# One expert product moved within the step of a fused attention and expert-mixture kernel

## Chip, cores and metric

The kernel runs on one NeuronCore of a Trainium2 chip. The metric is the device time of one execution in microseconds (us), as a median over runs; a separate profiled execution gives the trace. The engines are TensorE (PE: matrix products, with its weight loads shown as PEld), VectorE (DVE), ScalarE (ACT), GpSimd (POOL) and SyncE (SP, which here issues the DMAs). Each has its own queue and works it in order; engines meet through semaphores.

## What is computed

The input x is 2 images of 128 channels x 256 x 256 pixels in float32. One layer has two halves. The first is a dilated halo attention with four heads of 32 channels: in each window of 8 x 8 pixels the queries see a 12 x 12 surrounding, and a fixed mask leaves only the keys of the same parity. The second is a mixture of eight linear experts, of which the router takes two for each pixel.

```python
# attention half, on the channel-normalised x
qkv = einsum('bchw,oc->bohw', ln_c(x), W_qkv)
attn = softmax(q * SCALE @ k.T + rel_pos_emb(q) + FIXED_MASK)   # per window and head
x = x + einsum('bchw,oc->bohw', attn @ v, W_out)
# expert half, on every pixel as a token t of 128 channels
probs = softmax(ln_t(t) @ router_w + router_b)
top_p, top_i = top_k(probs, 2); top_p = top_p / sum(top_p)
t = t + sum_k top_p[k] * (ln_t(t) @ expert_w[top_i[k]] + expert_b[top_i[k]])
```

The kernel computes all eight experts for every pixel and multiplies each expert's input by its gate, which is zero for the six experts not taken; the eight products are summed in PSUM.

## The kernel before

An image is cut into strips of eight pixel rows, 64 strips for both images. The parity mask splits a strip into four planes (even or odd rows, even or odd columns) of 512 pixels, and attention is done plane by plane: 256 planes. The main loop (L779) has one step n for each plane and seven more to finish the experts. Within the loop the order of every engine's instructions is the order in which the Python code issues them (`manual_schedule`, L778); nothing is reordered afterwards.

A step interleaves four different pieces of work at different stages of a pipeline:
- `scores` (L436) and `attend` (L477) of plane n: the keys product (line 448, which adds position terms and mask) and the scores (line 465) into the PSUM tile `att`, an exponential on ACT (`pT`, line 473), sums (line 486) and weighted values (line 496), and on DVE a division that gives `o` (line 516).
- `project` (L357) of plane n+1, called `ahead` in the loop: first half of the values (`pvv`, line 369), position terms (`pu`, line 384), keys (`pk`, line 396), queries (`pq`, line 418), and later the second half of the values. The inputs come from the normalised strip `xn` and from window columns `xcol`, which POOL copies.
- `out_project` (L520) of plane n: the output product `po` (line 524), then on DVE the sum with the strip (line 529).
- `norms`, `route` and `spread` for a group of 512 pixels of the strip before: sums of squares by PE (line 554), a transpose `plg` and small operations on DVE, ACT's exponential (line 592), the choice of two experts by rank, and a write of the gates to DRAM (`gd`).

The experts belong to the class `Experts` (L644). `fetch` (L652) lets SP read a gate row back, broadcast over 128 partitions (256 KB), into a buffer `gb`; a one-column write on DVE or ACT ahead of it makes the DMA wait for the buffer. `times` (L673) multiplies the centred pixels `xs` with the gate and gives `xe`, for experts 0 to 4 and 6 on DVE and for 5 and 7 on POOL. `product` (L683) is the matmul of expert e into the PSUM tile `acc`, with 512 columns; in float32 it is two weight loads and two matmuls in the trace. `end` (L690) adds `acc` to the strip on DVE. `acc` has one buffer; `xe` has eight.

One group of 512 pixels spreads its eight products over two steps. In step n, after the second half of the values, come products 0, 1 and 2 (L848 to L851), then `po` (L862), then product 3 (L863). In step n+1, after keys, scores, first values, `pu`, `pk` and `pq`, come products 4, 6, 7 and 5 (L817). The variable `ex` is the group whose products run; it is replaced by the next group at L841, after the four products and `end`.

At the head of each step from the seventh on, L793 pads PE's instructions with idle ones, so that the step begins at a fixed place within a block of 256 instructions (`BLOCK` 256, `FIRST_LIMIT` 95, L47): the first 95 instructions of a step fall into one block and the next block begins after them. Small PSUM products share three buffers (`ps_mm`, L88).

Of the kernel before, what the change touches and what calls it, by code (L numbers as in the profile page):

```python
# [51 lines left out]
def kernel(  # L52
# [383 lines left out]
    def scores(n, state):  # L436


        qs, kk, au = state["qs"], state["kk"], state["au"]
        turn = place(n // 4, 0) // 2  # L440
        att = ps_att.tile([P, 4, 512], F32, tag="att", name=f"att{n}")
        sc = att[:, :, 0:HQ]
        for w in range(2):
            for half in range(2):
                rows = slice(half * SLOT, (half + 1) * SLOT)
                for h in range(HEADS):
                    hp = slice(h * DH, (h + 1) * DH)
                    nc.tensor.matmul(
                        sc[rows, h].rearrange("p (t w z) -> p t w z", w=2, z=16)[:, :, w],
                        lhsT=keys[hp, turn, w],  # L450
                        rhs=au[hp, half * NP + w : (half + 1) * NP : 2].rearrange(
                            "p t a s -> p t (a s)"
                        ),
                        start=(w == 0),
                        stop=False,
                    )
        for t in range(HP):
            if t == HP // 2:
                yield
            for half in range(2):  # L460
                rows = slice(half * SLOT, (half + 1) * SLOT)
                m0 = 2 * (half * HP + t)
                for h in range(HEADS):
                    hp = slice(h * DH, (h + 1) * DH)
                    nc.tensor.matmul(  # L465
                        sc[rows, h, 32 * t : 32 * t + 32],
                        lhsT=kk[hp, half * HP + t, :],
                        rhs=qs[hp, m0 : m0 + 2].rearrange("p m a s -> p (m a s)"),
                        start=False,
                        stop=(t == HP - 1),  # L470
                    )
        pT = work.tile([P, HEADS, HQ], F32, tag="pT", name=f"pT{n}", bufs=1)
        nc.scalar.activation(pT, att[:, :, 0:HQ], AF.Exp)  # L473
        state.update(att=att, pT=pT)
        yield

    def attend(n, state):  # L477


        att, pT, vv = state["att"], state["pT"], state["vv"]  # L480
        av = att[:, :, HQ:512]
        for half in range(2):
            rows = slice(half * SLOT, (half + 1) * SLOT)
            for h in range(HEADS):
                hp = slice(h * DH, (h + 1) * DH)
                nc.tensor.matmul(
                    av[hp, 2 + half], lhsT=ones[rows, :], rhs=pT[rows, h], start=True, stop=True
                )
        for t in range(HP):
            if t == HP // 2:  # L490
                yield
            for half in range(2):
                rows = slice(half * SLOT, (half + 1) * SLOT)
                for h in range(HEADS):
                    hp = slice(h * DH, (h + 1) * DH)
                    nc.tensor.matmul(  # L496
                        av[hp, half, 32 * t : 32 * t + 32],
                        lhsT=vv[rows, t, hp],
                        rhs=pT[rows, h, 32 * t : 32 * t + 32],
                        start=True,  # L500
                        stop=True,
                    )


        sT = work.tile([P, 2, HQ], F32, tag="sT", name=f"sT{n}", bufs=1)
        nc.vector.transpose(sT, av[:, 2:4])
        rc = small.tile([P, NQ // 32], F32, tag="rc", name=f"rc{n}")
        nc.vector.reciprocal(rc, sT.rearrange("p f (b k) -> p (f b) k", k=32)[:, :, 0])
        yield
        rT = work.tile([P, 2, HQ], F32, tag="rT", name=f"rT{n}", bufs=1)  # L510
        nc.vector.transpose(
            rT.rearrange("p f (b k) -> p (f b) k", k=32),
            rc.unsqueeze(2).broadcast_to([P, NQ // 32, 32]),
        )
        o = work.tile([P, 2, HQ], F32, tag="o", name=f"o{n}")
        nc.vector.tensor_tensor(o, av[:, 0:2], rT, ALU.mult)  # L516
        state["o"] = o
        yield

    def out_project(n, state):  # L520

        i, pl = divmod(n, 4)
        po = mm_tile(f"po{n}")
        nc.tensor.matmul(  # L524
            po, lhsT=wo, rhs=state["o"].rearrange("p f z -> p (f z)"), start=True, stop=True
        )
        yield
        xv = xt[i].rearrange("p (a y) (m s x) -> p y x m a s", y=2, x=2, s=4)[:, pl // 2, pl % 2]
        nc.vector.tensor_add(xv, po.rearrange("p (m a s) -> p m a s", a=PR, s=4), xv)
        yield  # L530
# [188 lines left out]
    def store(i, k):  # L719
        b, s = strips[i]  # L720
        r = s * R + 2 * k
        nc.sync.dma_start(out[b, :, r : r + 2, :], xt[i][:, 2 * k : 2 * k + 2, :])
        if k == R // 2 - 1:
            xt.pop(i)
# [48 lines left out]
    gated, ex, nxt = None, NoExperts(), NoExperts()  # L773
# [4 lines left out]
    with tc.manual_schedule(engines={ET.PE, ET.DVE, ET.Activation, ET.Pool, ET.SP}):  # L778
        for n in range(n_planes + 7):  # L779
            i, pl = divmod(n, 4)  # L780
            score, attn, outp, ahead, norm, rout = none, none, none, none, none, none
            if n < n_planes:
                score = scores(n, states[n])
                attn = attend(n, states[n])
                outp = out_project(n, states[n])
            if n + 1 < n_planes:
                states[n + 1] = {}
                ahead = project(n + 1, states[n + 1])

            if 6 <= n < n_planes:
                nc.tensor.addr_align(BLOCK, offset=BLOCK - FIRST_LIMIT)  # L793


            next(score, None)
            new, row = NoExperts(), None
            if gated and gated[0]:
                rout = route(*gated[0], *gated[2])
            next(rout, None)  # L800
            nxt.fetch(5, nc.scalar)
            for _ in rout:
                pass
            next(score, None)
            next(ahead, None)
            nxt.fetch(7, nc.scalar)
            if gated:
                f, c, made = gated
                gd, rb1 = spread(f, c, made[0], f"_{n}")
                row = (*c, rb1) if c else None  # L810
                new = Experts(*f, gd) if f else new
            next(ahead, None)
            if n + 1 < n_planes:
                states[n + 1]["shift"]()
            next(ahead, None)
            next(ahead, None)
            for e in (4, 6, 7, 5):  # L817
                ex.product(e)


            f = (i - 1, pl) if 0 < i <= len(strips) else None
            c = row_at(n)
            if f or c:
                norm = norms(f, c, f"_{n}")
            next(norm, None)
            next(attn, None)
            nxt.means()
            new.fetch_means()
            for e in (0, 1, 2, 3):
                nxt.times(e, dve)  # L830
            new.fetch(0, dve)
            for e in (4, 6):
                nxt.times(e, dve)
            new.fetch(1, dve)
            ex.end()
            new.fetch(2, dve)
            next(attn, None)
            next(attn, None)


            ex = nxt  # L841
            next(norm, None)
            load_x((n + 9) // 4, (n + 9) % 4, paced=True)
            new.fetch(3, dve)
            while to_store:
                store(*to_store.pop())
            next(ahead, None)
            ex.product(0)  # L848
            made = next(norm, None)
            ex.product(1)  # L850
            ex.product(2)  # L851
            new.fetch(4, nc.scalar)
            nxt.behind(6)
            nxt.times(5, pool)
            if row:
                ln1(*row, pool)
            if pl == 3 and i + 2 < len(strips):
                halo(i + 2)
            nxt.times(7, pool)
            if n + 2 < n_planes:  # L860
                columns(n + 2)
            next(outp, None)  # L862
            ex.product(3)  # L863
            next(outp, None)
            new.fetch(6, dve)
            gated, nxt = (f, c, made) if made else None, new
            states.pop(n, None)
# [58 lines left out]
```

The softmax here doesn't subtract the row's maximum and nothing guards it: scores larger than these inputs give would overflow.

## Time and profile before

| What | us |
|---|---|
| Median of 4 runs | 4485.49 |
| Lowest and highest of them | 4482.61, 4487.03 |
| The profiled execution's own time | 4482.61 |
| Its span in the trace | 4480.8 |
| PE busy | 4422.0 |
| DVE busy | 3997.3 |
| ACT busy | 1468.9 |
| POOL busy | 1319.7 |

The span is the time from the first to the last instruction in the trace. "Busy" is the time in which an engine had at least one instruction under way; ends of matmuls are modelled, so PE's figure is not the share of its peak. The granted PE clock was 0.998 on average. The timeline of one step shows the start in us from the span's start, the length of a merged group, engine, line, operation and tiles, and how many instructions were merged (two for each float32 product). One step, from the keys product of one plane to that of the next, goes from 2002.25 to 2019.41 us: 17.16 us. In it DVE is busy for 15.81 us, ACT for 5.87 us and POOL for 5.21 us.

The list of waits gives, for an instruction group, what it waited for, the total time, the number of waits and the longest. Lines with "issue" are times in which an engine waited for nothing that the trace shows. An instruction-queue line (q8) counts the packets with which the program itself is fetched.

### The profile page before, as it was taken

How to read it: one execution, taken by the hardware profiler on the slowest of the kernel's cores; microseconds unless marked ns; L12 is line 12 of the kernel's file. 1: busy time of each engine (PE TensorE's matmuls, PEld its weight loads, DVE VectorE, ACT ScalarE, POOL GpSimd, SP SyncE). 2: the span in 40 equal slices, each digit the busy share in tenths (PEclk: the TensorE clock that was granted, in tenths of full speed). 3: DMA queues.
4: the chain of work that ended last, by engine and by line, in shares of the span. 5: the costliest groups of instructions: out<-in, count | busy, mean ns of one | idle time of the engine just before them, and what ended most of it. 6: DMA issues, size and time to landing. Idle time of an engine off the chain costs nothing. (4 is left out here: it accounts for less than half of the span.)

```text
span 4480.8 us, 224632 instructions
## 1 busy us (share of the span) xinstructions
PE 4422.0 (99%) x96321; PEld 2681.4 (60%) x96321; DVE 3997.3 (89%) x11850; ACT 1468.9 (33%) x4022; POOL 1319.7 (29%) x1815
## 2 busy tenths in 40 slices
PE   7999999999999999999999999999999999999997
PEld 5666666666666666666666666666666666666653
DVE  5899999999999999999989999999999999999887
ACT  3333333333333333333333333333333333333321
POOL 1232323232323232332323232323232323232321
PEclk9999999999999999999999999999999999999999
DMA  2566666666656666666666666666666666666656
GB/s 82 176 191 185 192 184 192 185 192 185 193 184 193 184 192 185 191 188 189 187 188 187 189 188 188 190 185 192 184 193 185 192 183 194 186 192 184 192 164 187
DMA packets 519284, 828.12 MB, mean 185 GB/s; under 512 B 124186, under 2 KB 125850, under 8 KB 518298
## 3 DMA queue, kind: packets, MB, share of 16 engines
q1 hardware_dynamic: 517568, 813.46, 60.1%
q8 instruction: 769, 12.60, 1.1%
q14 instruction: 217, 1.78, 0.2%
q10 hardware_dynamic: 730, 0.29, 0.0%
HBM read 737.95 MB, written 75.56 MB: 182 GB/s over the span
## 5 line engine op out<-in xcount | busy, mean ns | idle before, releaser
L686 PE MATMUL acc<-xe,ew 128*128 128x512 f32 x4096 | 1890.0, 594 | 19.5 <-DVE gb L660 18.2
L686 PEld LDWEIGHTS acc<-xe,ew 128*128 128x128 f32 x4096 | 758.0, 190 | 887.4 <-issue 862.7
L677 DVE TENSOR_TENSOR xe<-xs,gb 128x512 f32<-128x512 f32 x1536 | 950.5, 686 | 11.2 <-PE acc L686 1.4
L681 POOL COPY last<-xe 128x1 f32<-128x1 f32 x256 | 48.3, 189 | 3058.2 <-DVE gb L660 3051.1
L376 ACT COPY vv<-pvv 128x512 f32<-128x512 f32 x512 | 300.2, 586 | 1396.4 <-PE pvv L369 1380.5
L677 POOL TENSOR_TENSOR xe<-xs,gb 128x512 f32<-128x512 f32 x512 | 651.1, 1273 | 5.6 <-PE att L496 2.1
L369 PE MATMUL pvv<-wt,xcol 128*128 128x128 f32 x4096 | 594.0, 288 | 2.5 <-POOL xcol L331 1.5
L369 PEld LDWEIGHTS pvv<-wt,xcol 128*128 128x128 f32 x4096 | 496.2, 191 | 64.7 <-issue 51.8
L272 POOL TENSOR_TENSOR xn<-xt,rb 128x512 f32<-128x512 f32 x249 | 375.2, 1507 | 69.1 <-DMA rb<-gd 60.6
L465 PE MATMUL att<-qs,kcol 32*64 32x32 f32 x32768 | 391.6, 226 | 1.0 <-issue 1.0
L465 PEld LDWEIGHTS att<-qs,kcol 32*64 32x64 f32 x32768 | 390.3, 130 | 1.2 <-issue 1.2
L496 PEld LDWEIGHTS att<-pT,vv 64*32 64x32 f32 x32768 | 348.1, 105 | 39.4 <-issue 2.7
L496 PE MATMUL att<-pT,vv 64*32 64x32 f32 x32768 | 343.1, 200 | 2.5 <-issue 2.5
L473 ACT ACTIVATE pT<-att 128x1024 f32<-128x1024 f32 x256 | 262.2, 1024 | 241.1 <-PE att L465 237.7
L548 ACT ACTIVATE sq<-xt 128x512 f32<-128x512 f32 x505 | 292.6, 630 | 0.0
L354 DVE STREAM_TRANSPOSE au<-auT 128x512 f32<-128x512 f32 x256 | 269.3, 1052 | 9.0
L524 PE MATMUL po<-o,wt 128*128 128x512 f32 x512 | 262.1, 593 | 6.2 <-DVE o L516 3.2
L418 PE MATMUL pq<-xn,wt 128*128 128x512 f32 x512 | 262.1, 593 | 0.4 <-issue 0.4
L384 PE MATMUL pu<-xn,wrel 128*128 128x512 f32 x512 | 262.3, 594 | 0.0
L407 ACT COPY kcol<-pk 128x560 f32<-128x560 f32 (+2 forms) x344 | 174.4, 507 | 267.7 <-PE pk L396 264.8
L396 PE MATMUL pk<-xn,wt 128*128 128x512 f32 (+2 forms) x528 | 261.0, 578 | 0.0
L386 DVE STREAM_TRANSPOSE uT<-pu 128x512 f32<-128x512 f32 x256 | 182.7, 714 | 75.6 <-PE pu L384 74.9
(2697 smaller groups left out, 5245.1 us busy)
## 6 DMA issues: line engine op xcount, KB each, us to landing
gb<-gd SPq DMA_DIRECT2D x2048, 256.0 KB, 4.1
xt<-in_x_dram SPq DMA_DIRECT2D x256, 256.0 KB, 5.0
sb<-gd SPq DMA_DIRECT2D x256, 256.0 KB, 3.6
out_dram<-xt SPq DMA_DIRECT2D x256, 256.0 KB, 4.3
rb<-gd SPq DMA_DIRECT2D x249, 256.0 KB, 3.4
gd<-gT SPq DMA_DIRECT2D x516, 16.0 KB, 3.0
ew<-in_L_ffn_expert_w_dram SPq DMA_DIRECT2D x1, 512.0 KB, 4.5
eb<-in_L_ffn_expert_b_dram SPq DMA_DIRECT2D x1, 512.0 KB, 5.6
```

What stands on the lines that cost most here:

```text
L272: eng.tensor_tensor(xn[i % 2][:, :, :, k, 1 : PC + 1], ln1_src(i, k).rearrange("p (y j x) -> p y x j", y=2, x=2), rb.rearrange("p (y j x) ...
L354: nc.vector.transpose(au.rearrange("p m a s -> p a s m"), auT[n % 2])
L369: nc.tensor.matmul(pv[:, t * P : (t + 1) * P], lhsT=xl[:, t0 + t].rearrange("p a k -> p (a k)"), rhs=wv, start=True, stop=True,)
L376: nc.scalar.copy(vv[:, t0 : t0 + 4, :].rearrange("p t c -> p (t c)"), pv)
L384: nc.tensor.matmul(pu, lhsT=wrel, rhs=inner, start=True, stop=True)
L418: nc.tensor.matmul(pq, lhsT=wq, rhs=inner, start=True, stop=True)
L465: nc.tensor.matmul(sc[rows, h, 32 * t : 32 * t + 32], lhsT=kk[hp, half * HP + t, :], rhs=qs[hp, m0 : m0 + 2].rearrange("p m a s -> p (m a ...
L473: nc.scalar.activation(pT, att[:, :, 0:HQ], AF.Exp)
L496: nc.tensor.matmul(av[hp, half, 32 * t : 32 * t + 32], lhsT=vv[rows, t, hp], rhs=pT[rows, h, 32 * t : 32 * t + 32], start=True, stop=True,)
L548: nc.scalar.activation(sq, src, AF.Square)
L677: eng.tensor_tensor(self.xe[e], self.xs, self.gb.pop(e), ALU.mult)
L686: nc.tensor.matmul(self.acc, lhsT=ew[:, e, :], rhs=self.xe.pop(e), start=(e == 0), stop=not self.xe)
```

## The change

Product 3 is no longer issued behind `po` in step n. It is issued in step n+1 ahead of products 4, 6, 7 and 5, behind `pq`. The group is the same: at that place `ex` still is the group of the step before. The order in which the eight experts are summed stays 0, 1, 2, 3, 4, 6, 7, 5. No other instruction changes its place in its engine's queue.

```diff
@@ -814,7 +814,7 @@
                 states[n + 1]["shift"]()
             next(ahead, None)
             next(ahead, None)
-            for e in (4, 6, 7, 5):
+            for e in (3, 4, 6, 7, 5):
                 ex.product(e)
 
 
@@ -860,7 +860,6 @@
             if n + 2 < n_planes:
                 columns(n + 2)
             next(outp, None)
-            ex.product(3)
             next(outp, None)
             new.fetch(6, dve)
             gated, nxt = (f, c, made) if made else None, new
```

## The prediction

> **What bounds the kernel now.** I read the page first, then the waits of TensorE (PE), then the timelines of PE, SP, ACT and DVE over two steps in the middle, and last the trace's single records.
>
> ```profile
> span 4480.8 us, 224632 instructions
> PE 4422.0 (99%) x96321; PEld 2681.4 (60%) x96321; DVE 3997.3 (89%) x11850; ACT 1468.9 (33%) x4022; POOL 1319.7 (29%) x1815
> ...
> L686 PE MATMUL acc<-xe,ew 128*128 128x512 f32 x4096 | 1890.0, 594 | 19.5 <-DVE gb L660 18.2
> ...
> q8 instruction: 769, 12.60, 1.1%
> ```
>
> A busy PE is partly a model, so its 99% is only a hint. The proof is the timeline of one step:
>
> ```profile
> 2016.74 1.02 PE L686 MATMUL acc<-xe,ew 128*128 128x512 f32 x2
> 2017.60 1.02 PE L524 MATMUL po<-o,wt 128*128 128x512 f32 x2
> 2018.46 1.02 PE L686 MATMUL acc<-xe,ew 128*128 128x512 f32 x2
> 2019.41 0.69 PE L448 MATMUL att<-au,keys 32*64 32x128 f32 x32
> 2019.90 1.53 PE L465 MATMUL att<-qs,kcol 32*64 32x32 f32 x128
> 2021.35 1.16 PE L369 MATMUL pvv<-wt,xcol 128*128 128x128 f32 x8
> 2022.35 1.02 PE L384 MATMUL pu<-xn,wrel 128*128 128x512 f32 x2
> 2023.21 1.02 PE L396 MATMUL pk<-xn,wt 128*128 128x512 f32 x2
> 2024.07 1.02 PE L418 MATMUL pq<-xn,wt 128*128 128x512 f32 x2
> 2024.93 3.59 PE L686 MATMUL acc<-xe,ew 128*128 128x512 f32 x8
> 2028.45 0.66 PE L486 MATMUL att<-pT,ones 64*32 64x256 f32 x16
> ```
>
> Every 512-column product takes a slot of 0.86 us (2017.60 to 2018.46, 2022.35 to 2023.21), and the next starts where it ends. Of the 255 intervals between the first L448 matmuls of neighbouring steps, 217 lie between 17.16 and 17.18 us. A step of 17.16 us that repeats this exactly is set by PE's own stream, not by a wait. The waits agree:
>
> ```profile
> PE acc L686 <- DVE gb L660: 18.2, 5, 5.0
> PE att L448 <- issue: 9.5, 8, 6.8
> PE po L524 <- DVE o L516: 3.2, 3, 1.1
> PE po L524 <- ACT vv L376: 2.0, 3, 0.7
> ```
>
> The 18.2 us come in five waits, in the last steps, where no attention is left. Away from the change of image in the middle, 227 steps exceed 17.161 us by 2.07 us in all; five longer steps at that change (127 to 130 and 132) exceed it by 2.0 us more. That is all that better cover could win in the steady part.
>
> **What is moved.** Product 3 is two weight loads and two matmuls, no DMA, no memset and no other engine's instruction. Before, it runs in the slot 2018.46, after the output product (po). After, po is followed at once by the keys and scores (L448, L465), the first half of the values (pvv), pu, pk and pq, and product 3 takes the slot after pq. On PE it passes the 32 + 128 matmul records of L448 and L465, eight of pvv, and pu, pk and pq; SP's, POOL's, ACT's and DVE's queues keep their order. Accumulation order stays 0,1,2,3,4,6,7,5. There are 256 such products; the last seven steps have nothing between the two places, so 249 really move.
>
> PE's work: 249 x (-0.86 + 0.86) = 0. The changes of shape are also as many as before: L448 starts 0.95 us after a 128x512 product starts (2018.46 to 2019.41), so 0.09 more than a slot, and the last product before L486 shows about the same. After the move po stands before L448 and has the same shape. I take 0 for this; the bounds are -0.09 and +0.09 us a step, -23 and +23 us.
>
> What follows is only whether a new wait arises, because everything from L448 to pq now starts 0.86 us earlier, while product 4 and all behind it keep their clock time. I put each releaser at its old time against the new need:
> - pu writes the buffer that po left; DVE's add (L529) releases it at 2018.66 + 0.69 = 2019.35. New need 2022.35 - 0.86 = 2021.49. Spare 2.1 us.
> - pk writes the buffer of DVE's plg; its last reader (L595) ends at 2003.60 in the slower of the two steps. Its weight load was at 2005.62, now 2004.76. Spare 1.2 us.
> - pq writes the buffer of pvv, emptied by ACT behind the exponential (pT). In the slower step ACT's routing exponential and a one-column copy hold it until 2003.65, so pT starts there, not at 2004.30 - 0.86 = 2003.44; 1.02 + 0.07 + 0.59 later the buffer is free, at 2005.33. pq's weight load comes at 2006.48 - 0.86 = 2005.62. Spare 0.29 us, and about 0.2 us in the latest steps. If that cover went by 0.2 us in a third of the steps it would cost 83 x 0.2 = 17 us. This is the tightest data wait. I take 0.
> - DVE's next xe3 now has to wait for product 3, which ends near 2025.1; DVE reaches that multiply near 2027.9. Spare 2.8 us. Behind it on DVE stand xe4, xe6, the add that empties acc (L692) and sT, and POOL and PE wait for those; nothing is late.
> - DVE waits for pu at uT (74.9 us in all, below). That wait can vanish, but DVE is pinned again by po and by the end of L496, so it brings nothing.
>
> ```profile
> DVE uT L386 <- PE pu L384: 74.9, 183, 7.1
> ```
>
> **PE's own instructions** are the remaining resource. They come in 16 KB blocks of 256 (769 packets; 2 x 96321 matmuls and loads plus 4312 others are 769 x 256). The alignment at L793 fixes the block edges at instructions 95, 351 and 607 of a step: in the scores, in the first expert behind pq, and in L496. Counted out (320 for keys and scores, 1 wait, 16 + 4 + 4 + 4), edge 351 lies between the two halves of product 4, and after the move between the halves of product 3. So its place after the start of L448 is the same. The records show that this edge is nearly critical: the load of that second half should start 5.52 us after L448; in a quarter of the steps it is late, and whenever it is late it starts 1.42 to 1.49 us after the end of one block's transfer. That transfer starts 1.45 to 3.96 us after L448 (median 2.9), takes 0.93 us, and may end 4.39 us after L448 before PE loses time (a load late by 0.35 us cost 0.03, by 0.45 us 0.13). What holds it up are the 256 KB gate broadcasts on SP, four in a row here:
>
> ```profile
> 2018.11 5.46 SPq L661 DMA_DIRECT2D gb<-gd  x4
> ```
>
> These follow DVE's routing and keep their clock time, so against L448 they come 0.86 us later. In the step where, by the records, they stood just so (each 0.88 us later than usual against L448), the transfer started at 1.56 us; in two steps where they stood 1.3 us later, at 1.45 and 3.37. None was late enough to cost. Where they stood 0.28 us later the median rose from 2.84 to 3.28. Bounds: gain 2 us (all lateness gone), loss by stretching that rise in a line: 0.44 / 0.28 x 0.86 = 1.35 us later, start 4.2, end 5.1, so 0.7 x 249 = 180 us. The nearest rows are the shifted steps, so I take 0. The block of edge 95 is fetched from about 12.6 us after L448 and loses 0.86 us of cover; the latest transfer of all (end 16.48) cost 0.09 us. After the move this costs some 1 us in the whole run.
>
> [...]
>
> **Sum.** 4480.8 (span) + 1.8 around it = 4482.6 for the profiled run; 0 for PE's work, 0 for waits, +1 for edge 95, -2 for edge 351: about 4482. The median of the runs is 2.9 above the profiled one, so 4485.
>
> **The rivals.**
> - *The block for edge 351 comes late, slower.* Later broadcasts push its transfer behind them. For it: the rise from 2.84 to 3.28. Against: the shifted steps. It decides once the transfer ends later than 4.39 us after L448. With one more such rise over the slower group (3.28 + 0.44 + 0.93 = 4.65) it costs 0.26 us in 249 steps, 65 us: 4550. Chance 0.20; with the pq wait (4502) slower has 0.24.
> - *The gap before L448 shrinks, faster.* If the 0.09 us belonged to the accumulating product and not to the change of shape, 249 x 0.09 = 23 us go: 4462. Against: L486 shows the same gap, and po differs only in its output. Chance 0.10.
> - *DVE sets the pace and gains its 74.9 us.* That would give 4411. Against: 17.16 us of PE without a gap while DVE works 15.5 to 15.8 of them. Under 0.01, counted with faster.
>
> **How the numbers follow.** No change has 0.66, with its own range 4479 to 4492 (runs 4482.6 to 4487.0, and -4 to +5 for the rests). About 0.2%, 9 us, is what a measurement of this kernel can tell from no change. Leaving out at most 2 in 10, the range reaches up into the late block, half-way to its price, and a little down: 4472 to 4532.
>
> **What would show it.** Right: steps of 17.16 us, L448 0.95 us after po, product 3 directly behind pq, DVE's wait at uT nearly gone, PE's waits as now. Wrong: a gap between the two halves of product 3 (late block), a wait of pq for ACT's vv, or of L448 or L465 for issue. A steady step other than 17.16 us by more than 0.035 makes the prediction wrong.

## The result and the profile after

The changed kernel takes 4495.23 us (median of 31 runs), the kernel before 4486.64 us (51 runs on the same chips). The ratio is 1.0018 with a 95% interval of 1.0013 to 1.0023: 6 to 10 us slower, 8.6 us by the medians. No change was forecast. The two profiled spans, 4480.8 and 4492.8 us, differ by more, 12.0 us: the stretches at half clock add up to 23 us in the profile before and to 42 us in the one after, nearly all of them in the first seven steps and from step 255 on.

The page after:

```profile
span 4492.8 us, 224884 instructions
PE 4428.1 (99%) x96321; PEld 2686.5 (60%) x96321; DVE 3918.5 (87%) x11850; ACT 1468.4 (33%) x4022; POOL 1320.7 (29%) x1815
...
L686 PE MATMUL acc<-xe,ew 128*128 128x512 f32 x4096 | 1849.8, 595 | 18.2 <-DVE gb L660 17.4
```

The busy times say little: the matmuls are as many, and PE is at 99% in both. The timeline of a regular step (start, length, engine, line, tiles, count) shows that the move does what it says:

```profile
2107.16 1.02 PE L524 MATMUL po<-o,wt 128*128 128x512 f32 x2
2108.11 0.69 PE L448 MATMUL att<-au,keys 32*64 32x128 f32 x32
2108.60 1.53 PE L465 MATMUL att<-qs,kcol 32*64 32x32 f32 x128
...
2112.77 1.02 PE L418 MATMUL pq<-xn,wt 128*128 128x512 f32 x2
2113.64 4.45 PE L686 MATMUL acc<-xe,ew 128*128 128x512 f32 x10
```

L448 stands 0.95 us behind po, and five products (x10) directly behind pq. The period of the regular step is still 17.16 us. The lost time is therefore in single steps. The first place is the last strip, steps 249 to 254, where no further strip has to be normalised. The timeline there, before (around L448 of step 250):

```profile
4301.82 1.02 PE L524 MATMUL po<-o,wt 128*128 128x512 f32 x2
4302.68 1.02 PE L686 MATMUL acc<-xe,ew 128*128 128x512 f32 x2
4303.91 0.70 PE L448 MATMUL att<-au,keys 32*64 32x128 f32 x32 [0.22 <-issue]
```

and after, around L448 of the same step and of the next:

```profile
4306.73 1.02 PE L524 MATMUL po<-o,wt 128*128 128x512 f32 x2
4308.77 0.70 PE L448 MATMUL att<-au,keys 32*64 32x128 f32 x32 [1.02 <-issue]
...
4314.28 4.45 PE L686 MATMUL acc<-xe,ew 128*128 128x512 f32 x10
...
4324.54 1.02 PE L524 MATMUL po<-o,wt 128*128 128x512 f32 x2
4326.69 0.70 PE L448 MATMUL att<-au,keys 32*64 32x128 f32 x32 [1.13 <-issue]
```

L448 waits for no data but for its own instruction ("issue"), 1.0 to 1.1 us where it was 0.2 (and up to 0.5 in the later steps of the strip). These steps lack 32 of PE's instructions (two of the four L554 groups), so L793 fills the next step's head with 46 idle instructions instead of 14. The trace's single records give their times. PE's instruction stream stands at a wait for `o` ahead of po. In step 249 before, that wait ends 3.54 us ahead of the next L448, the first idle instruction runs at -3.41 and the last at -0.07 us: 46 at 71 ns. In each of the six steps, in both profiles, L448 starts 0.07 us after the start of the last of them. In a regular step the 14 end 2.57 us ahead of L448 before and 1.72 us ahead after; there is slack.

So the last strip's steps are a loop: `o` released, 46 idle instructions (3.3 us), L448, scores, projections, the products behind pq, attention, `o`. Before, four products lay in that loop and product 3 ran beside the idle instructions. Now five lie in it. The six steps go from 17.00-17.07 to 17.68-17.92 us, and one of them to 19.33 us; the windows of steps 252 and 253 show why (window, length, busy times of PE, PEld, DVE, ACT and POOL with their instructions, granted PE clock, share of the DMA engines, GB/s):

```profile
4344.20:4361.80 17.60, 16.57 (x360) 10.01 (x360) 14.70 (x45) 4.92 (x13) 3.70 (x7) 1.00 0.53 151
4361.80:4381.20 19.40, 18.24 (x360) 11.12 (x360) 14.79 (x46) 4.92 (x13) 3.71 (x7) 0.91 0.52 141
```

The granted clock falls to 0.91 on average: 3.41 us at half clock, which the records place behind one of the 1.1 us gaps.

Three smaller places show up beside this one. At the head, the gap before L448 of step 7 (34 idle instructions behind po, before 30) is 2.06 us where it was 0.91, counted from the start of PE's last matmul. At the change of image (steps 127 to 130) pq waits for DVE's uT. And in a few regular steps the scores stop, here in step 202:

```profile
3483.65 0.35 PE L465 MATMUL att<-qs,kcol 32*64 32x32 f32 x15
3484.70 1.36 PE L465 MATMUL att<-qs,kcol 32*64 32x32 f32 x113 [0.70 <-issue]
```

The stop is behind 15 score matmuls and the 16th weight load: with the 64 instructions of L448 these are the 95 before the program's block edge. The block's transfer ended 0.12 us after L448 and the scores went on 1.42 us after that.

### The profile page after: what moved, and what is told of

It reads as the page before. It is cut to its first block, busy times and chain, and to the rows that moved or that the text cites. A ratio compares the mean times of both kernels' runs of the same rounds, so it can differ in the third digit from the quotient of the medians.

```text
span 4492.8 us, 224884 instructions
## 1 busy us (share of the span) xinstructions
PE 4428.1 (99%) x96321; PEld 2686.5 (60%) x96321; DVE 3918.5 (87%) x11850; ACT 1468.4 (33%) x4022; POOL 1320.7 (29%) x1815
## 5 line engine op out<-in xcount | busy, mean ns | idle before, releaser
L686 PE MATMUL acc<-xe,ew 128*128 128x512 f32 x4096 | 1849.8, 595 | 18.2 <-DVE gb L660 17.4
L496 PEld LDWEIGHTS att<-pT,vv 64*32 64x32 f32 x32768 | 348.2, 105 | 40.1 <-issue 3.3
L496 PE MATMUL att<-pT,vv 64*32 64x32 f32 x32768 | 343.2, 200 | 3.1 <-issue 3.1
L592 ACT ACTIVATE lg<-lg 128x32 f32<-128x32 f32 x256 | 58.7, 229 | 609.9 <-DVE lg L591 609.9
```

Of the source, the lines that this page charges most:

```text
L496: nc.tensor.matmul(av[hp, half, 32 * t : 32 * t + 32], lhsT=vv[rows, t, hp], rhs=pT[rows, h, 32 * t : 32 * t + 32], start=True, stop=True,)
L686: nc.tensor.matmul(self.acc, lhsT=ew[:, e, :], rhs=self.xe.pop(e), start=(e == 0), stop=not self.xe)
```

## The experiments

All were timed beside the kernel before. In all but the last two the loop uses a function `late(m)` that says for which step's group product 3 is moved (the edit against the kernel before):

```diff
+            if late(n - 1):
+                ex.product(3)
             for e in (4, 6, 7, 5):
                 ex.product(e)
...
             next(outp, None)
-            ex.product(3)
+            if not late(n):
+                ex.product(3)
             next(outp, None)
```

**The last strip alone.** `late(m)` is `249 <= m <= 254`.

> Product 3 is moved only for the groups of steps 249 to 254, everywhere else it stays behind po. Theory (idle instructions): in these six steps PE's sequencer has 46 idle instructions of 71 ns each, 3.3 us, between the release of po and L448; product 3 covered 0.86 us of them, so each step grows from 17.00-17.07 to 17.7-17.9 us and the run from the time before by 4 to 6 us (ratio 1.0009 to 1.0013), nearly all of the measured loss; every other step as before. Rival (head and tail): the loss of 8.6 us comes from before step 7 and after step 255, where the changed profile also was 3.5 and 2.0 us longer; then this run is within 2 us of before and steps 249 to 254 matter little.

Measured: 4492.95 against 4486.44 us, ratio 1.0013 (1.0004 to 1.0022). The steps take 17.34, 17.83, 17.70, 17.70, 17.83 and 17.68 us; their sum is 106.1 us against 102.3. Six steps out of 249 places make a large part of the loss: 6.5 us by the medians, 3.8 us in this profile; the interval covers both. The stretches at half clock can explain the difference. The runs of this kernel had a mean granted clock of 0.9955, those of the kernel before 0.9964, and of the 81 runs of the kernel before in all the experiments those at 0.995 averaged 4491.4 us and those at 0.997 4484.9; that is 3.2 us for each 0.001, so by estimate some 3 of the 6.5 us.

**Everything but the last strip.** `late(m)` is `not 249 <= m <= 254`.

> Product 3 is moved everywhere but for the groups of steps 249 to 254. Theory: steps 249 to 254 are back at 17.0-17.1 us, steady steps stay at 17.16 us, the four steps at the change of image keep their extra 1 us, so the run is 0 to 3 us above the time before (ratio 1.0000 to 1.0007). Rival (head and tail): 6 to 9 us above before, as the whole change.

Measured: 4490.87 us, 1.0008 (1.0000 to 1.0017): above my 0 to 3 us, below the rival's. The last strip is back at 16.98 to 17.07 us (its first step 17.60). Something besides it costs.

**The idle instructions moved, in the changed kernel and in the kernel before.** Steps 249 to 254 get 32 of the 46 behind their products. 369 instructions of the step lie ahead of that place with five products behind pq; in the kernel before, with four, it is 365:

```diff
                 ex.product(e)
+            if 249 <= n <= 254:
+                nc.tensor.addr_align(BLOCK, offset=(BLOCK - FIRST_LIMIT + 369 + 32) % BLOCK)
```

> The whole change, but in steps 249 to 254 32 of the 46 idle instructions come behind product 5 instead of at the head of the next step; the block edges in the next steps stay where they were. Theory: at that place PE's array still has several us of products queued, so the idle instructions are hidden; L448 follows po by 0.95 us again and the six steps fall to about 16.7 us (17.16 less the 0.43 us by which L554 is shorter there), below the 17.0-17.1 of before. The run comes to 1 us below to 2 us above before (ratio 0.9998 to 1.0005). Rival (DVE or the gates set these steps once product 3 is gone): the steps stay at 17.7-17.9 us and the run 6 to 9 us above before.

> The kernel before, with the same 32 idle instructions behind product 5 in steps 249 to 254. Theory: the six steps fall from 17.00-17.07 to about 16.7 us, the run by about 2 us (ratio 0.9993 to 0.9999), since before only 0.3 us a step of the idle instructions was uncovered. Rival: steps stay at 17.0-17.1 us, ratio 1.

Measured: 4486.63 us, 1.0001 (0.9993 to 1.0010), and 4484.52 us, 0.9996 (0.9987 to 1.0005, which holds no change). In the first, L448 of the last strip is 0.95 us behind po:

```profile
4311.28 1.02 PE L524 MATMUL po<-o,wt 128*128 128x512 f32 x2
4312.23 0.69 PE L448 MATMUL att<-au,keys 32*64 32x128 f32 x32
...
4317.75 4.45 PE L686 MATMUL acc<-xe,ew 128*128 128x512 f32 x10
```

The six steps take 16.51 to 16.73 us, 99.5 us in all against 108.1 in the changed kernel, with the same five products behind pq. In the second they take 16.51 to 16.96 us, 100.2 in all against 102.3 before. This shows the idle instructions as the cause there.

**The regular steps alone, and the head with the change of image.** `late(m)` is `m >= 7 and not 126 <= m <= 129 and not 249 <= m <= 254`, and `m == 6 or 126 <= m <= 129`.

> Product 3 is moved for every group but those of steps 6, 126 to 129 and 249 to 254, so in 236 of the 249 places. Theory (the loss sits in the few irregular steps): the run equals before, within 1.5 us either way (ratio 0.9997 to 1.0003), and steady steps stay at 17.16 us. Rival (the steady steps lose a little each through late program blocks or half-speed clock): 3 to 6 us above before.

> Product 3 is moved only for the groups of step 6 and of steps 126 to 129. Theory: the gap before L448 of step 7 grows from 0.9 to 2.06 us (34 idle instructions with no product over them), and with it a longer stretch at half clock; in steps 127 to 130 pq waits for DVE's uT, about 0.45 us each, some 1.2 us in all against the steps before; together 2 to 4 us above before (ratio 1.0004 to 1.0009). Rival (only the last strip matters): within 1 us of before.

Measured: 4489.34 us, 1.0005 (0.9996 to 1.0014), and 4490.76 us, 1.0007 (0.9998 to 1.0016). Neither is settled by its time: 2.8 us above before lies between my 1.5 and the rival's 3, and 4.2 us just above my 2 to 4. The traces say more. In the first, the regular steps exceed 17.161 us by 6.3 us, 5.3 of them stops at edge 95. This is the highest of the profiles with the new order (table below), but the theory of a neutral regular step is wrong by a few us. In the second, the gap before L448 of step 7 is 2.06 us, and pq waits in each of steps 127 to 130. The wait, as the changed kernel shows it:

```profile
2196.88 1.24 PE L396 MATMUL pk<-xn,wt 128*128 128x512 f32 x4
2198.30 1.13 PE L418 MATMUL pq<-xn,wt 128*128 128x512 f32 x2 [0.19 <-DVE uT L386]
```

These steps make the keys in two parts (x4), so the three small PSUM buffers rotate one further, and pq takes the one that uT has to leave.

**All idle instructions moved.** Beside the ones above, 103 of the 104 at the head of step 6 go ahead of the program's first product, and 16 behind pq in step 6 (in the changed kernel 20, with 369 in place of 365 and, as above, 369 + 32):

```diff
+    nc.tensor.addr_align(BLOCK, offset=168)
     pw = mm_tile("pw")
...
+            if n == 6:
+                nc.tensor.addr_align(BLOCK, offset=(BLOCK - FIRST_LIMIT + 365) % BLOCK)
+            if 249 <= n <= 254:
+                nc.tensor.addr_align(BLOCK, offset=(BLOCK - FIRST_LIMIT + 365 + 32) % BLOCK)
```

> The kernel before (product 3 behind po) with the idle instructions put where PE has nothing to do or has products queued: 104 of them before PE's first transpose instead of at the head of step 6, 16 behind pq in step 6, 32 behind product 5 in steps 249 to 254. Theory (idle instructions at 71 ns each are real time on PE's path where nothing covers them): step 5 falls from 19.9 us to 12.5 to 14 us, step 6 by 0.4 us, steps 249 to 254 to 16.5 to 16.9 us, the run by 6 to 10 us (ratio 0.9978 to 0.9987). Rival: another wait (gates, DVE) stands behind the idle ones at step 6 and the run falls by 2 to 3 us only, as with the last strip alone.

> The whole change with the same idle instructions moved. Theory: the place of product 3 is nearly neutral once no idle instruction is uncovered; the run is 0 to 2 us above e8_idle_moved (the 1.2 us of the change of image remain), 5 to 9 us below before. Rival (the order itself costs): 5 us or more above e8_idle_moved.

Measured: 4480.79 us, 0.9985 (0.9976 to 0.9993), and 4481.40 us, 0.9989 (0.9980 to 0.9997), against 4486.52. The first is 5.7 us below before, just short of my 6 to 10. The kernel with product 3 behind po and the idle instructions moved is faster than both kernels of this study. Before, in step 5:

```profile
106.05 1.12 PE L524 MATMUL po<-o,wt 128*128 128x512 f32 x2 [0.68 <-ACT vv L376]
113.92 1.16 PE L448 MATMUL att<-au,keys 32*64 32x128 f32 x32 [6.75 <-issue]
```

and with the idle instructions moved (lines are one further down):

```profile
108.60 1.12 PE L525 MATMUL po<-o,wt 128*128 128x512 f32 x2 [0.68 <-ACT vv L377]
109.65 0.69 PE L449 MATMUL att<-au,keys 32*64 32x128 f32 x32
```

Step 5 falls from 19.86 to 13.02 us, and 3.5 us of it come back in step 6 (20.33 against 16.83), where PE stops for issue three times, 1.1, 1.3 and 2.2 us. The idle instructions are not free at the start either: the first product waits longer there, before

```profile
PE pw L166 <- DVE wall L160: 6.2, 1, 6.2
```

and with them moved

```profile
PE pw L167 <- issue: 8.5, 1, 8.5
```

With next to nothing idle in the way, the two orders differ by 0.6 us of 4481, which the intervals do not separate. They do not exclude the 3.6 us of the second and third row of the table below either: in the profile of the second kernel steps 127 to 130 take 71.4 us (70.2 in the first), and edge 95 still stops the scores.

**Another product between po and L448.** Product 2 behind po in place of ahead of it, with five still behind pq; or product 4 behind po and four behind pq (edits against the changed kernel):

```diff
-            ex.product(2)
             new.fetch(4, nc.scalar)
...
             next(outp, None)
+            ex.product(2)
             next(outp, None)
```

```diff
-            for e in (3, 4, 6, 7, 5):
+            for e in (3, 6, 7, 5):
...
             next(outp, None)
+            ex.product(4)
             next(outp, None)
```

> The whole change, but product 2 now stands behind po instead of ahead of it, so a product again lies between po and L448, while five still stand behind pq. Theory (what counts is how much of PE's work lies between the attention, which releases o and the late program blocks, and the next L448; that work is as short as in the changed kernel): steps 249 to 254 stay at 17.6-17.9 us, the program block at edge 95 is late in some steps as in the changed kernel, the run is 5 to 10 us above before (ratio 1.0011 to 1.0022). Rival (L448 directly behind po is what costs): steps 249 to 254 are back at 17.0-17.1 us, no late block at edge 95, within 2 us of before.

> The whole change, but product 4 takes the place that product 3 left behind po, so four products stand on either side as before and only experts 3 and 4 have changed places. Theory: the number of products between the attention and L448 decides, not which expert it is; steps 249 to 254 at 17.0-17.1 us, no late block at edge 95, no wait of pq at the change of image, within 2 us of before (ratio 0.9996 to 1.0004). Rival (the later end of product 3 delays DVE's next xe3 or the order of the sums matters): 3 us or more above before.

Measured: 4505.25 us, 1.0046 (1.0033 to 1.0058), and 4484.86 us, 0.9999 (0.9990 to 1.0008), against 4485.01. The last strip with product 2 behind po:

```profile
4319.43 1.02 PE L524 MATMUL po<-o,wt 128*128 128x512 f32 x2
4320.29 1.02 PE L686 MATMUL acc<-xe,ew 128*128 128x512 f32 x2
4322.40 0.70 PE L448 MATMUL att<-au,keys 32*64 32x128 f32 x32 [1.09 <-issue]
```

A product stands between po and L448 and the wait is there all the same; steps of 17.69 to 18.13 us (one at half clock for a while, 19.55). So what counts is not what follows po but how many products lie in the loop between L448 and `o`. With four on either side, whichever expert it is, the steps of the last strip take 16.98 to 17.06 us and nothing is lost:

```profile
4306.17 1.02 PE L524 MATMUL po<-o,wt 128*128 128x512 f32 x2
4307.03 1.02 PE L686 MATMUL acc<-xe,ew 128*128 128x512 f32 x2
4308.27 0.70 PE L448 MATMUL att<-au,keys 32*64 32x128 f32 x32 [0.23 <-issue]
```

The further 10 us with product 2 behind po I had not forecast: the block of edge 351 is late in 104 of 232 regular steps, which exceed 17.161 us by 14.0 us together. The late block at edge 95 that I had forecast for that kernel came in one step alone, 0.2 us. With that order po, and so DVE's sum and routing and the gate broadcasts behind it, come earlier against the attention; that these delay the block is argued, not shown.

## Why the prediction was wrong

**The step that failed** is the multiplication "249 x (-0.86 + 0.86) = 0" with the list of releasers behind it. Both were worked out on the regular step and taken for all 249 places. L793 was read only as what fixes the block edges; the idle instructions that it adds were not counted as work on PE's path. In six steps there are 46 of them, and product 3 was what covered 0.86 us of their 3.3 us. Even the kernel before showed it, in the wait of L448 for issue in the last strip. Such a wait was among the prediction's own signs of being wrong; it grew from 9.5 us in all before to

```profile
PE att L448 <- issue: 13.9, 8, 5.8
```

The measured 4495 us lies within the stated 4472 to 4532 by luck: the range reached that far up for a late block at edge 351, and that block came earlier (below). It lies above the 4479 to 4492 given for no change, and the 8.6 us, taken beforehand as too small to tell from no change, could be told with 31 and 51 runs.

What the runs put in its place, from the profiles (sums in us; old order: product 3 behind po at the place in question; new order: moved):

| Place | old order | new order | difference of means |
|---|---|---|---|
| Steps 249 to 254, sum (5 and 3 profiles) | 102.1 to 102.8 | 106.1 to 108.6 | 5.2 |
| 226 regular steps, excess of the longer ones over 17.161 (6 and 5) | 0.6 to 2.9 | 1.7 to 6.3 | 2.3 |
| Steps 127 to 130, sum (5 and 4) | 69.8 to 70.5 | 71.4 to 71.5 | 1.3 |
| Gap before L448 of step 7 (5 and 4) | 0.88 to 0.92 | 2.06 | 1.2 |

They add to 10 us, at the upper end of the measured 6 to 10. The first row includes two stretches at half clock of some 1.7 us each, and where only some groups are moved step 249 holds a product more or less (some 0.5 us). The changed kernel's own profile shows nothing lost in the second row: 1.7 us, with 2.0 before. The order with product 2 behind po counts in the first row alone.

**The regular step** stays at 17.16 us with L448 0.95 us behind po: right. (Its count of PE's instructions, said to be 769 x 256, comes to 196954, which is 90 more; the places of the edges do not hang on it.) The gap of 0.09 us before L448 is there behind po as it was behind product 3 (0.95 us from start to start in both), and the rival that would have gained it fell.

**The data waits** were right for the regular step: pq did not wait there. The tightest one did break at another place and through another buffer, at the change of image, in four waits:

```profile
PE pq L418 <- DVE uT L386: 0.8, 4, 0.2
```

**DVE's wait for pu** went, and brought nothing, as forecast. Before, DVE waited little for the end of L496 and for po:

```profile
DVE sT L506 <- PE att L496: 11.6, 12, 2.8
DVE xt L529 <- PE po L524: 5.3, 19, 0.5
```

The waits after:

```profile
DVE sT L506 <- PE att L496: 84.0, 246, 3.2
DVE xt L529 <- PE po L524: 77.4, 178, 1.1
DVE uT L386 <- PE pu L384: 30.7, 13, 6.9
```

The 74.9 us at uT fell to 30.7 and DVE now waits for the end of L496 and for po.

**The block of edge 351**, my slower rival, did the opposite: its transfer starts 2.45 us after L448 (median; 2.92 before), and its load is late in 15 of 232 steps instead of 59. The reading from the few shifted steps at the start was right, and of the 2 us put down as gain most came: the excess of the regular steps before (2.0 us) stands nearly all in steps with this block late, and of the 1.7 us after all but some 0.4 are stops at edge 95. The rival's cost exists, as product 2 behind po shows, but not in this change. That the gate broadcasts hold this transfer up was my inference and was not shown: in the changed kernel two of the broadcasts issued around L448 stand 0.86 us later against it (medians 0.85 and 1.95 us after L448, -0.01 and 1.10 before), and the transfer starts 0.47 us earlier.

**The block of edge 95** was the mechanism with the wrong size: I took 1 us, the five profiles show 1.3 to 5.3 us. I had given it 0.86 us less cover; its transfer in fact starts 14.4 us after the L448 before (median) where it was 12.6, so 1.8 us are gone. Why it starts a further 1 us later is open.

**The fetch of the blocks** does matter here. Behind edge 95 the three stops of the changed kernel (steps 26, 94 and 202) ended 1.43 to 1.49 us after the end of that very block's transfer; at edge 351 the late loads before started 1.20 to 1.59 us after it (median 1.44), a wider range than the 1.42 to 1.49 of the prediction. In these steps the block was not there ahead of its use.

The granted clock differs from run to run (0.995 to 0.998 in the 81 runs of the kernel before), but over many runs hardly between the two kernels: its mean is 0.9963 for the changed kernel and 0.9964 for those 81 runs. At 3.2 us for each 0.001 that is under 1 us of the 8.6, by estimate.

## What to carry to other kernels

A move that is neutral in the step that repeats has to be worked through once more in the steps that differ: first, last, and those where a row or a part is missing. Idle instructions that align code were work on the engine's instruction stream here; look at what runs beside them and put them where the engine has products queued. In the last strip, where a loop of waits set the pace, what counted was how many products lay inside that loop (four: 17.00 to 17.07 us a step before, five: 17.68 to 17.92 in the changed kernel, and one of 19.33 with half clock in it), not which one, nor next to what.

## What the runs showed of the hardware

- An idle instruction took 71 ns of PE's instruction stream (median from start to start, step 249 before); 46 of them set the pace of a 17 us step in the last strip, and 103 moved away took 6.8 us off step 5.
- PE's 196954 instructions came in 769 packets of 16384 bytes, 256.1 to a packet. The transfer of the block of edge 351 took 0.95 us before (median), and a late load started 1.20 to 1.59 us after its end; one late by 0.45 us cost 0.13. At edge 95 in step 202 of the changed kernel the scores went on 1.42 us after the end of the transfer (0.70 us without a matmul).
- In the last strip PE was granted half its clock for 3.41 us in two of the 18 steps that began with a gap of 1.0 to 1.4 us (one in the changed kernel, one with product 2 behind po); it cost 1.6 to 1.8 us each time. Between step 8 and the last strip, where such gaps are missing, neither the profile before nor the one after shows half clock.
